# Two residual bottleneck layers on one core: VectorE's and GpSimd's order written out in one stage, beds for the kept rows, and a third term added by VectorE in another

## The chip, the cores and the metric

The kernel is one program on one core of a Trainium2 chip. The time is that of the device in microseconds; lower is better. The kernel before took 1981.97 us, the median of three runs (1979.57 to 1982.63). The profile is of one further execution.

## The reference

The input has 64 images of 1024 channels and 14 x 14 pixels, in fp32. Two layers of the same form follow each other:

```python
out = relu(bn(conv1x1(x, w1, b1)))        # 1024 -> 256 channels
out = relu(bn(conv3x3(out, w2, b2)))      # 256 -> 256
out = bn(conv1x1(out, w3, b3))            # 256 -> 1024
x = relu(x + softplus(residual_scale) * out)
```

`bn` takes mean and variance of its own input over all images and pixels, channel by channel. So no layer's result can be normalized before the whole of it, or its statistics in another way, is known.

## The kernel before

**Tiles.** Two images make a tile: 32 tiles of 392 pixels. With 128 channels on the partitions a tile of the wide tensor has 8 rows of 392 values (one row is 128 x 392), a tile of the narrow tensor 2. Tiles 16 to 31 are called kept, since their conv3 results are stored to memory (`zs`) before the normalization is known. The narrow tensor of all tiles stays on chip in `y_all`; `two(t, s)` is its area of tile t and half s.

**Products.** conv1 and conv3 use seven block products in place of eight (class `Seven`, with `Conv1` and `Conv3`). The seven, p1 to p7, use sums of weight blocks and sums t1 to t4 of the input's blocks, and their results are put together from banks of the accumulator: p1 starts a bank y, which is copied by ScalarE (`after1`), takes p6 and is copied again (`after6`), takes p7, and, in Conv3, is copied once more (`after7`, cu3). The banks are called ay, ap, ax for conv1, cy, cp, cx for conv3. `stream` puts the products of neighbouring units into this order: p1 of the unit, p3 and p4 of the unit before, p6, then `end` of the unit before, p2, p5, p7. (Conv1 has p4 before p3.) One step of a stream is two matmuls of 196 columns; a tile of conv1 has 28 steps, a unit of conv3, which makes two rows of a tile, has 7. Where the text speaks of products it means such steps.

**Stages,** by their place in the span: conv1 of the first layer (0 to 330 us); its 3 x 3 convolution, tile after tile with transformed weights (to 585); the **mixed** stage (585 to 811); the **fused** stage (811 to 1327); the 3 x 3 convolution of the second layer (to 1605); its statistics (to 1690) and the final conv3 with the residual (to 1985).

**Mixed** takes statistics of conv3's output by products of the narrow tensor with itself for tiles 0 to 15 (moves by DMA, transposes on VectorE at L1193), and makes conv3 of tiles 16 to 31 itself: class `Direct`, 60 units of two rows. A unit's row is put together in a tile `kept` and stored to `zs` by SyncE; `bn_stats` of its two rows stand in `end` (L568). In `Direct` the third term of the second row is copied from the bank by ScalarE to cu3 and added by GpSimd (L521, `after7` of `Conv3`).

**Fused** ends the first layer and makes conv1 of the second. Three generators run interleaved. *a* is conv1 of the second layer, 32 tiles in the order of `positions()`: even places are tiles 0 to 15, odd places are kept tiles. *c* is conv3 of the first layer for the tiles at even places, 60 units; one step of c follows two of a, with a start of 14 steps of c. *kept_rows* gives the 16 kept tiles their residual, row by row, 128 rows; one row every 7 steps of a, so two in a unit. Row r is loaded from `zs` by SyncE (`bring`) into a bed, a part of `y_all`, 8 rows ahead; rows 104 and later come through two beds in the raw weights, 2 ahead. Even rows of a tile are multiplied and added by VectorE in one instruction (L1689); odd rows by GpSimd in two (L1686, L1687). Then ScalarE does the relu with the shift in place. A row of a conv3 tile gets from VectorE the adds from banks cp, cy and cx (L500), from GpSimd the adds of cu12 (L526) and cu3 (L521), then the relu.

On VectorE a tile of conv1 has the block sums t3, t2, t1 (L432, L433, L434, 128 x 784) once its p1 is recorded and t4 (L451) after p6, the results (L420) and `bn_stats` (L423); each conv3 tile has four column sums (L463 to L466).

**What sets the order.** Each engine runs its instructions one after the other in a fixed list. Instructions under `tc.keep_in_program_order` stand in that list in the order in which the program records them; others are placed by a scheduler before the kernel is built. TensorE's matmuls, ScalarE's activations (`act`, L332) and SyncE's loads are under it in the fused stage; VectorE's and GpSimd's instructions there are not.

Of the kernel before, what the change touches and what calls it, by code (L numbers as in the profile page):

```python
# [69 lines left out]
def bottlenecks(ctx: ExitStack, tc: tile.TileContext, x, w1s, w2s, w3s, pars, out):  # L70
# [259 lines left out]
    def act(*args, **kw):  # L330

        tc.keep_in_program_order(nc.scalar.activation(*args, **kw))  # L332

    class Conv1(Seven):


# [37 lines left out]
        def end(self):  # L374
            pass
# [47 lines left out]
                self.run(nc.vector.bn_stats(self.stats[:, o, self.at[i % len(self.at)], :], whole), o, i)  # L423

        def run(self, ins, o, i):
            if self.pinned:
                tc.keep_in_program_order(ins)

        def after1(self):
            self.u1 = self.saved("au1")  # L430
            self.t1, self.t2, self.t3 = (self.sum(i) for i in range(1, 4))
            nc.vector.tensor_sub(self.t3, self.b[1][1], self.b[0][1])  # L432
            nc.vector.tensor_add(self.t2, self.t3, self.b[0][0])  # L433
            nc.vector.tensor_sub(self.t1, self.b[0][1], self.b[0][0])  # L434

        def after2(self):
            self.result(0, 0, self.x, self.u1)
# [10 lines left out]
        def after6(self):  # L448
            self.u2 = self.saved(*("au2",) if self.border is None else ("au4",) if len(self.ts) > 1 else ("cu3",))
            self.t4 = self.sum(4)  # L450
            nc.vector.tensor_sub(self.t4, self.b[1][0], self.t2)  # L451

        def after7(self):
            self.result(1, 1, self.p, self.saved("au3"))
# [1 line left out]
    def column_sums(pool, ys, n, twice=(2, 3), eng=nc.vector):  # L456

        sums = []
        for i in range(4):
            v = pool.tile([P, n], FP, tag=f"ct{i}", name=f"ct{i}", bufs=1 + (i in twice))  # L460
            sums.append(v.rearrange("p (h l) -> p h l", l=G * W))
        t1, t2, t3, t4 = sums
        eng.tensor_sub(t3, ys[1][1], ys[0][1])  # L463
        eng.tensor_add(t2, t3, ys[0][0])
        eng.tensor_sub(t1, ys[0][1], ys[0][0])
        eng.tensor_sub(t4, ys[1][0], t2)  # L466
        return sums

    class Conv3(Seven):
# [27 lines left out]

        def add(self, row, i, bank):
            o, v = self.o[row], self.part(row, i)
            nc.vector.scalar_tensor_tensor(v, bank, self.scale[:, o : o + 1], v, ALU.mult, ALU.add)  # L500

        def relu(self, row):
            o = self.o[row]
# [14 lines left out]

        def after7(self):
            u3 = self.saved(self.pool.tile([P, self.n], FP, tag="cu3", name="cu3", bufs=self.thirds), 1)  # L520
            nc.gpsimd.tensor_add(self.part(1, 1), self.part(1, 1), u3)  # L521

        def after3(self):
            self.add(0, 1, self.p)
            v = self.xt[:, self.o[0], :]
            nc.gpsimd.tensor_add(v, v, self.u12)  # L526

        def after4(self):
            self.add(1, 0, self.y)
# [1 line left out]
        def end(self):  # L531
            for row in range(2):
                self.relu(row)
            if self.to is not None:
                nc.scalar.dma_start(out=self.to, in_=self.xt.rearrange("p s f -> p (s f)"))

    class Direct(Conv3):

        thirds = 2

# [806 lines left out]
    def positions():  # L1347
        return [KEPT * (p % 2) + p // 2 for p in range(T)]

    def bed(r):  # L1350

        if r >= ROWS[1]:
            return None
        g, i = (NG - 3, NG - 1)[r >= ROWS[0]], r % AHEAD
        a = g * GPX + i % 4 * PX
        return y_all[:, i // 4, a : a + PX]

    def bring(to, r):

        t, o = KEPT + r // CS, r % CS  # L1360
        if t < T:
            tc.keep_in_program_order(nc.sync.dma_start(out=to, in_=zs[t - KEPT][:, o * PX : (o + 1) * PX]))

    def mixed(psum, pool, one, x_right, x_left, aff, minus_c, w3, made_c, summed_c, summed_a, mv3, xs, coming_x):

# [134 lines left out]
        places = positions()  # L1500
        for k, _ in enumerate(stream(units(), total, together=True)):
            unit, step = divmod(k, 7)
            t, q = KEPT + 1 + unit // 4, unit % 4
            if step == 0 and q == 0 and t + 1 < T:
                coming = prepare(t + 1)
            if step == 3:
                if q < 2:
                    next(coming, None)
                if q > 0:
                    next(norms, None)  # L1510
                if unit in moves:
                    move(moves[unit])
                if unit in (21, 25, 29, 33):
                    next(summed_a)
                if unit in (44, 48):
                    coming_x()
                if 50 <= unit < 50 + AHEAD:
                    bring(bed(unit - 50), unit - 50)
            if step == 5 and q == 1:
                next(coming, None)  # L1520
            if step == 2 and unit == at[0]:
                grams = batches()
            if step == 2 and unit in at or step == 5 and unit - 1 in at or step == 2 and unit - 2 in at:
                next(grams, None)
            if step == 6 and unit > at[-1] + 1:
                if tail is None:
                    assert next(grams, "end") == "end"
                    tail = conv3_stats(
                        psum, pool, (upper, lower, by, gs), w3, mv3,
                        ("ay", "ay", "ap", "ax"), homes[1], ("ay", "ay", "ay"),  # L1530
                    )
                next(tail, None)
        assert next(tail, "end") == "end"
        for _ in range(3):
            coming_x()
# [115 lines left out]
            unit.go_out()  # L1651
        residual(psum, xs[T - 1], 1, T - 1, a, aff)

    def fused(psum, pool, one, coming, xs, raw, w1, w3, aff, par, stats, border, begun):

# [4 lines left out]
        scale, shift = aff  # L1660
        n = PX // 2
        places = positions()
        beds = raw[0][:, 1, 0].rearrange("p s m -> p (s m)"), raw[1][:, 0, CS // 2 :].rearrange("p s m -> p (s m)")
        beds = [v[:, :PX] for v in beds]

        def at(r):
            return beds[r % 2] if bed(r) is None else bed(r)

        def last_convs():
            for p in range(2, T, 2):  # L1670
# [6 lines left out]
        def first_convs():  # L1677
            for p, t in enumerate(places):
                yield Conv1(psum, pool, xs[p : p + 1], (t,), w1, par, stats, border, (p,))

        def kept_rows():

            for r, (p, o) in enumerate(itertools.product(range(1, T, 2), range(CS))):
                v, z = xs[p][:, o, :], at(r)
                if o % 2:
                    nc.gpsimd.tensor_scalar(z, z, scale[:, o : o + 1], None, ALU.mult)  # L1686
                    nc.gpsimd.tensor_add(v, v, z)  # L1687
                else:
                    nc.vector.scalar_tensor_tensor(v, z, scale[:, o : o + 1], v, ALU.mult, ALU.add)  # L1689
# [6 lines left out]
                yield  # L1696

        a, c, rows = stream(first_convs(), T), stream(last_convs(), (KEPT - 1) * CS // 2), kept_rows()
        done = LAG
        for i in range(LAG):  # L1700
            next(c)
            if i == 2:
                for run in begun:
                    run()
            if i % 3 == 1:
                next(rows)
        for k in itertools.count():
            p, step = divmod(k, 28)
            if step == 14 and 0 < p < T - 4:
                assert len(xs) == p + 4  # L1710
                coming(4)
            if k % 7 == 3:
                next(rows, None)
            if next(a, "end") == "end":
                break
            while done < LAG // 2 + (k + 1) // 2:
                next(c, None)
                done += 1
        assert next(c, None) is None and next(rows, None) is None

    def stats_tile(n, name):
        return keep.tile([P, n, T, nc.vector.BN_STATS_DIM], FP, tag=f"stats{n}", name=name)
# [200 lines left out]
    for b in range(2):  # L1923
# [9 lines left out]
        with tc.tile_pool(name=f"last_{b}", bufs=1, **({"reuse_waits": "tile"} if b == 0 else {})) as one, tc.tile_pool(  # L1933
# [12 lines left out]
            with ExitStack() as scope:  # L1946
# [53 lines left out]
                with tc.tile_pool(name=f"rest_{b}", bufs=1) as pool:  # L2000
                    if b == 1:
                        final(psum, pool, [x_left] * 5 + [more], xs, w3, *weights, aff)
                        return
                    stats1 = stats_tile(MS, f"stats1_{b + 1}")
                    border = Border(b + 1, stats1, x_scope)
                    fused(psum, pool, one, coming, xs, (w1, w3), *weights, aff, par[b + 1], stats1, border, later)


# [38 lines left out]
```

## Time and profile before

| what | us |
|---|---|
| median of three runs | 1981.97 |
| the profiled execution | 1986.55 |
| its span, first to last instruction | 1984.7 |
| mixed stage, TensorE busy | 210.95 of 226.00 |
| fused, 811 to 850, TensorE busy | 34.18 of 39.00 |
| fused, 850 to 1150, TensorE busy | 283.89 of 300.00 |
| fused, 1150 to 1313, TensorE busy | 134.64 of 163.00 |
| 1313 to 1605, TensorE busy | 289.48 of 292.00 |

The profile writes PE for TensorE, PEld for its weight loads, DVE for VectorE, ACT for ScalarE, POOL for GpSimd, SP for SyncE. A timeline row has start, duration, engine, line, operation, output and input, count, and in brackets the idle time of the engine ahead of it with what ended it. Starts of rows on one engine can be closer than the durations, since one instruction begins while the one before drains. L numbers are lines of the kernel; the line of a helper stands for all that it records (L159 every matmul, L332 every activation).

### The profile page before, as it was taken

What the parts mean: (1) busy time and instruction counts of PE and PEld (TensorE: products, weight loads), DVE (VectorE), ACT (ScalarE), POOL (GpSimd) and SP (SyncE); (2) the same over time, 40 slices, a digit from 0 to 9 for tenths busy, and PEclk for the clock granted to TensorE, in tenths of its full rate; (3) what the DMA queues carried; (4) which work ended last, traced back from release to release, by engine and by line L of the source; (5) the groups of instructions that cost most, each with busy time, mean ns of one, the idle gap of its engine ahead of it and who ended that gap; (6) DMA issues with size and microseconds to landing.
All of it is one profiled execution on the core that took longest, in us unless ns stands there. A gap on an engine that the chain in (4) does not pass through costs nothing. (4 is left out here: it accounts for less than half of the span.)

```text
span 1984.7 us, 28827 instructions
## 1 busy us (share of the span) xinstructions
PE 1909.2 (96%) x9778; PEld 1576.8 (79%) x9778; DVE 1591.7 (80%) x2458; ACT 1097.2 (55%) x2283; POOL 752.6 (38%) x801
## 2 busy tenths in 40 slices
PE   9999999999998999999999997799999999999999
PEld 5555558999986788799999997789999987555555
DVE  5778669999985666888888875469999988788886
ACT  2222215777766655555455553236777783666666
POOL 0111100112125555666666644501211141667665
PEclk9999999999999999999999998899999999999999
DMA  7776735879745545777677765437787747699997
GB/s 285 280 254 237 256 122 161 223 205 222 213 142 159 159 144 203 276 272 279 260 264 272 276 235 212 159 130 212 202 225 207 204 132 257 258 324 336 344 357 277
DMA packets 246356, 458.22 MB, mean 231 GB/s; under 512 B 41344, under 2 KB 212960, under 8 KB 233152
## 3 DMA queue, kind: packets, MB, share of 16 engines
q1 hardware_dynamic: 208976, 374.23, 55.5%
q0 software_dynamic: 31616, 31.07, 7.6%
q10 hardware_dynamic: 5616, 51.06, 6.2%
q8 instruction: 78, 1.28, 0.3%
q14 instruction: 70, 0.57, 0.1%
HBM read 289.44 MB, written 141.03 MB: 217 GB/s over the span
## 5 line engine op out<-in xcount | busy, mean ns | idle before, releaser
L332 ACT ACTIVATE cu<-cy,scale 128x196 f32<-128x196 f32 (+1 forms) x360 | 178.9, 502 | 276.5 <-PE cy L159 274.6
L159 PE MATMUL columns<-v,ub 128*128 128x224 f32 (+1 forms) x1536 | 302.3, 338 | 1.1 <-ACT columns L332 0.8
L332 ACT ACTIVATE x<-x,shift 128x392 f32<-128x392 f32 x452 | 259.8, 612 | 51.2 <-POOL x L526 30.4
L159 PEld LDWEIGHTS columns<-v,ub 128*128 128x128 f32 x1536 | 268.8, 188 | 6.8 <-ACT columns L332 1.5
L159 PE MATMUL ay<-at,ws 128*128 128x196 f32 (+1 forms) x768 | 195.9, 387 | 2.6 <-ACT au L332 2.6
L159 PEld LDWEIGHTS ay<-at,ws 128*128 128x128 f32 x768 | 139.4, 194 | 37.4 <-ACT au L332 2.9
L500 DVE SCALAR_TENSOR_TENSOR x<-cp,scale,x 128x196 f32<-128x196 f32 (+1 forms) x240 | 124.1, 517 | 51.9 <-PE cp L159 50.4
L583 POOL TENSOR_TENSOR x<-x,cu 128x392 f32<-128x392 f32 x120 | 125.8, 1049 | 72.9 <-DVE x L500 71.4
L521 POOL TENSOR_TENSOR x<-x,cu 128x196 f32<-128x196 f32 (+1 forms) x120 | 121.9, 1016 | 74.6 <-ACT cu L332 66.0
L159 PE MATMUL l<-diffs,ub 128*128 128x224 f32 (+1 forms) x768 | 149.6, 337 | 0.3 <-ACT sd L1762 0.3
L159 PE MATMUL m<-sums,ua 128*128 128x224 f32 (+1 forms) x752 | 146.0, 336 | 0.2 <-DVE sums L699 0.2
L332 ACT ACTIVATE au<-ay 128x196 f32<-128x196 f32 (+1 forms) x140 | 53.2, 380 | 157.1 <-PE ay L159 149.3
L159 PEld LDWEIGHTS l<-diffs,ub 128*128 128x128 f32 x768 | 134.6, 189 | 1.2 <-ACT sd L1762 0.6
L159 PE MATMUL ap<-x,ws 128*128 128x196 f32 (+1 forms) x360 | 99.8, 410 | 37.1 <-DVE y L420 37.1
L159 PEld LDWEIGHTS m<-sums,ua 128*128 128x128 f32 x752 | 131.5, 189 | 1.4 <-DVE sums L699 0.8
L159 PE MATMUL cx<-y,w 128*128 128x196 f32 (+1 forms) x396 | 123.6, 398 | 3.5 <-DVE kept L555 3.4
L159 PE MATMUL cy<-y,w 128*128 128x196 f32 (+1 forms) x404 | 125.0, 397 | 0.0
L159 PE MATMUL cy<-ct,wt 128*128 128x196 f32 x480 | 122.7, 338 | 1.4 <-ACT cu L332 1.4
L332 ACT ACTIVATE y<-y,shift,scale 128x1568 f32<-128x1568 f32 (+7 forms) x102 | 118.7, 1183 | 6.6 <-DVE shift L1794 6.5
L997 POOL DMA_DIRECT2D y<-f x24 | 32.4, 1664 | 232.3 <-DVE f L917 232.3
L159 PE MATMUL cy<-ct,w 128*128 128x196 f32 (+1 forms) x360 | 114.1, 399 | 1.3 <-ACT cu L332 1.3
L159 PEld LDWEIGHTS ap<-x,ws 128*128 128x128 f32 x360 | 68.9, 206 | 58.0 <-DVE y L420 37.0
(298 smaller groups left out, 4448.7 us busy)
## 6 DMA issues: line engine op xcount, KB each, us to landing
ub<-u SPq DMA_DIRECT2D x92, 768.0 KB, 5.4
x<-in_x SPq DMA_DIRECT2D x35, 1568.0 KB, 8.2
x<-mid SPq DMA_DIRECT2D x32, 1568.0 KB, 8.9
mid<-x ACTq DMA_DIRECT2D x31, 1568.0 KB, 6.2
out<-x SPq DMA_DIRECT2D x123, 392.0 KB, 7.9
x<-in_x SPq DMA_DIRECT2D x108, 392.0 KB, 4.5
z<-kept SPq DMA_DIRECT2D x64, 392.0 KB, 3.0
ua<-u SPq DMA_DIRECT2D x92, 256.0 KB, 3.1
```

Source lines behind the costliest of these rows:

```text
L159: tc.keep_in_program_order(nc.tensor.matmul(*args, **kw))
L332: tc.keep_in_program_order(nc.scalar.activation(*args, **kw))
L500: nc.vector.scalar_tensor_tensor(v, bank, self.scale[:, o : o + 1], v, ALU.mult, ALU.add)
L521: nc.gpsimd.tensor_add(self.part(1, 1), self.part(1, 1), u3)
L583: nc.gpsimd.tensor_add(v, v, self.u12[:, i * self.n : (i + 1) * self.n])
L997: nc.gpsimd.dma_start(out=out_rows[3][:, o], in_=fa[:, o, :full], accum_op=ALU.add)
```

## The change

1. **Fused, order.** A list `pinned` is filled at the stage's start and emptied at its end; a helper `run` and the method `Conv1.run` put VectorE's and GpSimd's instructions under `keep_in_program_order` while it is filled. This takes in the sums, results and statistics of conv1, the column sums, the adds of conv3 and the kept rows.
2. **Fused, beds.** `bed(r)` becomes `beds(spare)`, which gives each row its bed and the row after which it is asked for. Rows 104 to 119 use the two old beds and a ring of areas of `y_all` whose tiles are done, so the eight rows of a tile are asked for together; the eight rows of the last tile come as one load into a tile `whole`.
3. **Mixed.** `Direct.after7` adds the third term straight from the bank on VectorE; cu3 and the GpSimd addition go. `bn_stats` of a unit's second row is put off to the next unit's `after7`.

The lines move: L420 to L427, L423 to L430, L432, L433, L434 to L439, L440, L441, L451 to L458, L500 to L507, L521 to L528, L526 to L533, L561 to L568, L568 to L579, L1686, L1687, L1689 to L1723, L1724, L1726. The new addition in mixed is L574.

```diff
+    pinned = []
+    def run(ins):
+        if pinned:
+            tc.keep_in_program_order(ins)
...
         def run(self, ins, o, i):
-            if self.pinned:
+            if self.pinned or pinned:
                 tc.keep_in_program_order(ins)
...
-            nc.vector.tensor_sub(self.t3, self.b[1][1], self.b[0][1])
+            run(nc.vector.tensor_sub(self.t3, self.b[1][1], self.b[0][1]))
...
     class Direct(Conv3):
-        thirds = 2
...
+        def after7(self):
+            nc.vector.tensor_add(self.part(1, 1), self.y, self.part(1, 1))
+            while waiting:
+                waiting.pop()()
+        def stat(self, row):
+            nc.vector.bn_stats(self.stats[:, self.o[row], self.t - KEPT, :], self.z[:, row])
         def end(self):
-            for row in range(2):
-                nc.vector.bn_stats(self.stats[:, self.o[row], self.t - KEPT, :], self.z[:, row])
+            self.stat(0)
+            waiting.append(partial(self.stat, 1))
...
+    def beds(spare):
+        places, before, last = [], {}, {}
+        for r in range((T - KEPT - 1) * CS):
+            t, o = KEPT + r // CS, r % CS
+            if r < ROWS[1]:
+                g, i = (NG - 3, NG - 1)[r >= ROWS[0]], r % AHEAD
+                a = g * GPX + i % 4 * PX
+                key, v = (g, i), y_all[:, i // 4, a : a + PX]
+            else:
+                ring = [(u, s) for s in range(MS) for u in range(t, T)]
+                i = o - MS
+                key = ("spare", o % MS) if i < 0 or i >= len(ring) else ring[i]
+                v = spare[key[1]] if key[0] == "spare" else two(*key)
+            places.append(v)
+            if key in last:
+                before[r] = last[key]
+            elif r >= ROWS[1]:
+                before[r] = ROWS[1] - 1
+            elif r >= AHEAD:
+                before[r] = r - AHEAD
+            last[key] = r
+        return places, before
...
             for r, (p, o) in enumerate(itertools.product(range(1, T, 2), range(CS))):
-                v, z = xs[p][:, o, :], at(r)
+                v, z = xs[p][:, o, :], at[r] if r < len(at) else whole[0][:, o]
                 if o % 2:
-                    nc.gpsimd.tensor_scalar(z, z, scale[:, o : o + 1], None, ALU.mult)
-                    nc.gpsimd.tensor_add(v, v, z)
+                    run(nc.gpsimd.tensor_scalar(z, z, scale[:, o : o + 1], None, ALU.mult))
+                    run(nc.gpsimd.tensor_add(v, v, z))
...
                 act(v, v, AF.Relu, bias=shift[:, o : o + 1])
-                for ahead in AHEAD, 2:
-                    if (r + ahead < ROWS[1]) == (ahead == AHEAD):
-                        bring(at(r + ahead), r + ahead)
+                for q in behind[r]:
+                    bring(at[q], q)
...
+            if step == 14 and p == T - 4:
+                whole.append(right.tile([P, CS, PX], FP, tag="x", name="whole"))
+                tc.keep_in_program_order(
+                    nc.sync.dma_start(out=whole[0].rearrange("p s f -> p (s f)"), in_=zs[T - 1 - KEPT])
+                )
```

More of the change, by code (lines that the diff above doesn't have):

```diff
@@ L450, in after6 @@
             self.t4 = self.sum(4)
-            nc.vector.tensor_sub(self.t4, self.b[1][0], self.t2)
+            run(nc.vector.tensor_sub(self.t4, self.b[1][0], self.t2))
         def after7(self):
@@ L462, in column_sums @@
         t1, t2, t3, t4 = sums
[L463 to L466, printed above, removed]
+        run(eng.tensor_sub(t3, ys[1][1], ys[0][1]))
+        run(eng.tensor_add(t2, t3, ys[0][0]))
+        run(eng.tensor_sub(t1, ys[0][1], ys[0][0]))
+        run(eng.tensor_sub(t4, ys[1][0], t2))
         return sums
@@ L499, in add @@
             o, v = self.o[row], self.part(row, i)
-            nc.vector.scalar_tensor_tensor(v, bank, self.scale[:, o : o + 1], v, ALU.mult, ALU.add)
+            run(nc.vector.scalar_tensor_tensor(v, bank, self.scale[:, o : o + 1], v, ALU.mult, ALU.add))
         def relu(self, row):
@@ L520, in after7 @@
             u3 = self.saved(self.pool.tile([P, self.n], FP, tag="cu3", name="cu3", bufs=self.thirds), 1)
-            nc.gpsimd.tensor_add(self.part(1, 1), self.part(1, 1), u3)
+            run(nc.gpsimd.tensor_add(self.part(1, 1), self.part(1, 1), u3))
         def after3(self):
@@ L525, in after3 @@
             v = self.xt[:, self.o[0], :]
-            nc.gpsimd.tensor_add(v, v, self.u12)
+            run(nc.gpsimd.tensor_add(v, v, self.u12))
         def after4(self):
@@ L1361, in bring @@
         if t < T:
-            tc.keep_in_program_order(nc.sync.dma_start(out=to, in_=zs[t - KEPT][:, o * PX : (o + 1) * PX]))
+            z = zs[t - KEPT][:, o * PX : (o + 1) * PX]
+            z = z if len(to.shape) == 2 else z.rearrange("p (h l) -> p h l", h=H)
+            tc.keep_in_program_order(nc.sync.dma_start(out=to, in_=z))
     def mixed(psum, pool, one, x_right, x_left, aff, minus_c, w3, made_c, summed_c, summed_a, mv3, xs, coming_x):
@@ L1499, in mixed @@
         at = [5, 9, 13, *range(16, 46, 3)]
-        places = positions()
+        at_first, _ = beds((None, None))
         for k, _ in enumerate(stream(units(), total, together=True)):
@@ L1517, in mixed @@
                 if 50 <= unit < 50 + AHEAD:
-                    bring(bed(unit - 50), unit - 50)
+                    bring(at_first[unit - 50], unit - 50)
             if step == 5 and q == 1:
@@ L1532, in mixed @@
                 next(tail, None)
+        waiting.pop()()
         assert next(tail, "end") == "end"
@@ L1652, in final, with fused @@
         residual(psum, xs[T - 1], 1, T - 1, a, aff)
-    def fused(psum, pool, one, coming, xs, raw, w1, w3, aff, par, stats, border, begun):
+    def fused(psum, pool, one, right, coming, xs, raw, w1, w3, aff, par, stats, border, begun):
         scale, shift = aff
@@ L1662, in fused @@
         places = positions()
[L1663 to L1667, printed above, removed]
+        spare = raw[0][:, 1, 0].rearrange("p s m -> p (s m)"), raw[1][:, 0, CS // 2 :].rearrange("p s m -> p (s m)")
+        at, before = beds([v[:, :PX] for v in spare])
+        behind = collections.defaultdict(list)
+        for r, q in before.items():
+            behind[q].append(r)
         def last_convs():
@@ L1696, in kept_rows @@
                 yield
+        whole = []
+        pinned.append(True)
         a, c, rows = stream(first_convs(), T), stream(last_convs(), (KEPT - 1) * CS // 2), kept_rows()
@@ L1702, in fused @@
             if i == 2:
-                for run in begun:
-                    run()
+                for late in begun:
+                    late()
             if i % 3 == 1:
@@ L1719, in fused @@
         assert next(c, None) is None and next(rows, None) is None
+        pinned.clear()
     def stats_tile(n, name):
@@ L2005, in bottlenecks @@
                     border = Border(b + 1, stats1, x_scope)
-                    fused(psum, pool, one, coming, xs, (w1, w3), *weights, aff, par[b + 1], stats1, border, later)
+                    fused(psum, pool, one, x_right, coming, xs, (w1, w3), *weights, aff, par[b + 1], stats1, border, later)
 def kernel(**inputs):
```

15 lines of the change are left out of this document (6 added, 9 removed).

## The prediction

> **What bounds the kernel now.** First the page's span, busy shares and, for later, one row of its DMA issues (count, KB, us to landing); then the windows, which give the same by stage; the columns are PE, weight load, VectorE, ScalarE, GpSimd, granted clock, DMA share and GB/s.
>
> ```profile
> span 1984.7 us, 28827 instructions
> ...
> PE 1909.2 (96%) x9778; PEld 1576.8 (79%) x9778; DVE 1591.7 (80%) x2458; ACT 1097.2 (55%) x2283; POOL 752.6 (38%) x801
> ...
> x<-in_x SPq DMA_DIRECT2D x35, 1568.0 KB, 8.2
> ```
>
> ```profile
> 585.00:811.00 226.00, 210.95 (x1327) 176.26 (x1326) 150.00 (x340) 129.90 (x361) 119.29 (x158) 0.98 0.52 168
> ...
> 850.00:1150.00 300.00, 283.89 (x1688) 280.87 (x1686) 244.08 (x421) 159.34 (x361) 191.41 (x159) 0.99 0.73 269
> 1150.00:1313.00 163.00, 134.64 (x709) 131.28 (x708) 96.18 (x186) 67.18 (x152) 71.78 (x63) 0.88 0.51 185
> ```
>
> TensorE is the bound nearly everywhere; only where it idles can a change win, and only work put on its path can lose. The diff touches two stages. Mixed (585 to 811) leaves TensorE idle for 226.00 - 210.95 = 15.05 us in all. Fused is told best by its products. These are its first and last rows on TensorE, and around 1026 the products of conv3 (two records each):
>
> ```profile
> 816.59 0.49 PE L159 MATMUL cy<-y,w 128*128 128x196 f32 x2
> ```
>
> ```profile
> 1325.47 1.49 PE L159 MATMUL ay<-x,ws 128*128 128x196 f32 x8
> ```
>
> ```profile
> 1026.93 0.49 PE L159 MATMUL cp<-y,wt 128*128 128x196 f32 x2
> ...
> 1031.91 0.49 PE L159 MATMUL cy<-ct,wt 128*128 128x196 f32 x2
> ...
> 1032.90 0.49 PE L159 MATMUL cy<-y,w 128*128 128x196 f32 x2
> ...
> 1033.90 0.49 PE L159 MATMUL cp<-y,wt 128*128 128x196 f32 x2
> ...
> 1039.56 0.49 PE L159 MATMUL cp<-ct,wt 128*128 128x196 f32 x2
> ```
>
> The interleave is one conv3 product after two of conv1, so between the rows at 1026.93 and 1031.91 lie five conv3 and ten conv1 products: 4.98 / 15 = 0.332 us for each. The stage has 60 units of 7 conv3 products and 32 tiles of 28 conv1 products, 420 + 896 = 1316, or 437 us; it lasts 1325.47 + 1.49 - 816.59 = 510.4. So **about 73 us are lost**. The waits of the steady part (850 to 1150) and of the late part (1150 to 1310), as total, times, longest, say where:
>
> ```profile
> PE ap L159 <- DVE y L420: 16.1, 10, 2.5
> ...
> ACT x L332 <- POOL x L526: 8.9, 24, 0.5
> ```
>
> ```profile
> DVE x L1689 <- DMA w<-z: 29.2, 11, 6.5
> POOL w L1686 <- DMA w<-z: 27.7, 10, 6.9
> ...
> PE ap L159 <- DVE y L420: 20.0, 6, 7.2
> ```
>
> Steady: a stall of 1.6 us once in two tiles, 16.1 in all. Late: VectorE and GpSimd wait for the rows that come through two beds, TensorE behind them (20.0 there), and the clock falls: (1 - 0.88) x 163 = 20 us. The rest, some 17, is the stage's start and single gaps.
>
> **The change, part by part.**
>
> *The beds (fused).* Eight areas instead of two let rows 104 and later be asked for early, and the last tile comes whole. This takes the late waits away: 20.0 of stalls, some 20 of clock and a few single gaps, up to 45 us. On SyncE's queue it moves the eight loads and the whole tile's ahead of what used to stand between them. The eight are asked for only when row 103 is done: the longest late wait for a bed, 6.9 us, is the nearest row, so 0 to 7 us once. The whole tile, 1568 KB, lands after some 8.2 us by the page's row of that size; its first use is ten conv1 products on, 15 products or 5.0 us at today's pace, so 0 to 3 us once. I take 0 for both, since the parts below leave each load more time than it has now.
>
> *The pinned order (fused).* TensorE's and ScalarE's orders here are the same as before, so what counts is what stands ahead of what on VectorE and GpSimd. Here is one unit on GpSimd and on ScalarE as it runs now:
>
> ```profile
> 1029.98 1.26 POOL L1686 TENSOR_SCALAR y<-y,scale 128x392 f32<-128x392 f32 x1
> 1031.33 1.50 POOL L1687 TENSOR_TENSOR x<-x,y 128x392 f32<-128x392 f32 x1
> 1032.81 1.98 POOL L1686 TENSOR_SCALAR y<-y,scale 128x392 f32<-128x392 f32 x1
> ...
> 1038.00 1.02 POOL L526 TENSOR_TENSOR x<-x,cu 128x392 f32<-128x392 f32 x1 [0.42 <-DVE x L500]
> ```
>
> ```profile
> 1029.45 0.42 ACT L332 ACTIVATE cu<-cy,scale 128x196 f32<-128x196 f32 x1 [2.05 <-PE cy L159]
> ...
> 1031.44 0.33 ACT L332 ACTIVATE au<-ay 128x196 f32<-128x196 f32 x1 [0.40 <-PE cp L159]
> ...
> 1038.10 0.42 ACT L332 ACTIVATE cu<-cy,scale 128x196 f32<-128x196 f32 x1 [3.07 <-PE cy L159]
> 1039.05 1.13 ACT L332 ACTIVATE x<-x,shift 128x392 f32<-128x392 f32 x2 [0.53 <-POOL x L526]
> ```
>
> Now two odd kept rows run one after the other on GpSimd (L1686 at 1029.98 and again at 1032.81). They run ahead of need: ScalarE's relu of an odd row stands in its fixed order between the two copies of a unit into cu12, and no wait of that relu for L1687 is in either list above; its only GpSimd wait is for L526 (8.9 us, relus at a unit's end). In the recorded order each unit has on GpSimd: the add of cu3, the add of cu12 of the unit before (L526, new L533), then the odd row's multiplication and addition (new L1723, L1724). On ScalarE: first cu12 copy, relu of that same row, second cu12 copy. TensorE may not put the seventh product on bank cy until the second copy has read it. A loop closes, once in each of the 60 units:
>
> p3 on cp, then VectorE's add from cp (L507), GpSimd's L533, L1723, L1724, ScalarE's relu and second copy, then p7.
>
> TensorE leaves 4.98 us from p3 to p7 (1026.93 to 1031.91). The loop, by rows:
>
> ```profile
> 1030.98 0.97 DVE L434 TENSOR_TENSOR at<-x 128x784 f32<-128x784 f32 x1
> ...
> 1032.53 1.13 DVE L432 TENSOR_TENSOR at<-x 128x784 f32<-128x784 f32 x1
> 1033.59 0.95 DVE L1689 SCALAR_TENSOR_TENSOR x<-y,scale,x 128x392 f32<-128x392 f32 x1
> 1034.46 0.96 DVE L433 TENSOR_TENSOR at<-at,x 128x784 f32<-128x784 f32 x1
> ...
> 1037.05 0.55 DVE L423 BATCH_NORM_STATS2 stats<-y 128x6 f32<-128x392 f32 x1
> 1037.53 0.40 DVE L500 SCALAR_TENSOR_TENSOR x<-cp,scale,x 128x196 f32<-128x196 f32 x1
> ...
> 1040.09 0.42 DVE L500 SCALAR_TENSOR_TENSOR x<-cp,scale,x 128x196 f32<-128x196 f32 x1 [0.57 <-PE cp L159]
> ```
>
> The row at 1039.56 on TensorE that released 1040.09 is the same step as p3: 0.53 from a product's start to the add's. The add takes 0.40 and GpSimd starts 0.07 later (1037.53, 1038.00); L533 1.02, L1723 1.26, L1724 1.02 as L526 of the same shape, 0.13 between them; relu 0.5 (half of a pair's 1.13), copy 0.42, with 0.11 of hand-overs. Sum **5.5 us**, 0.5 more than there is, with GpSimd undisturbed. The rows at 1032.81 and 1031.33 are the high end: 1.98 and 1.50, so 6.7.
>
> *Two halves of a tile.* That is the half in which the add from cp is next on VectorE. In the other half its recorded place is behind the three column differences of the next conv1 tile. From the moment R at which the second copy ends, ScalarE does two relus (1.1) and au3 (0.33; with a store's issue between in some, 0.4 more). VectorE's first instruction there waits for au3; then come, at the starts' spacing of the rows, result 0.33, two adds 0.66, kept row 0.62 to 0.95, three differences 0.9 to 1.1 each, statistics 0.5 and the add from cp 0.41: 5.2 to 5.8. So the add ends at R + 6.7 to 7.2, and the loop from there (L533 on) takes 4.5 to 5.7: this half lasts 11.2 to 12.9 us, where TensorE needs 7.0. In the first half p3 starts two steps of 1.0 us after p7, so R + 2.0 + 5.5 = 7.5 to 9.1.
>
> *Clock.* A long gap also costs rate afterwards:
>
> ```profile
> 1202.79 1.65 PE L159 MATMUL ap<-x,ws 128*128 128x196 f32 x4 [3.19 <-DVE y L420]
> ```
>
> ```profile
> 1066.43 0.93 PE L159 MATMUL ap<-x,ws 128*128 128x196 f32 x4 [2.49 <-DVE y L420]
> ```
>
> Four records took 1.65 us after a gap of 3.19, but 0.93 after one of 2.49. A gap of 4 to 6 us in each tile would so halve the rate for some 5 us; where the loop, not TensorE, sets the time, only the 2.0 us from p7 to p3 grow, to 4.0. I take 0 to 2 us for a tile and 0.7, because the gap may come in two pieces. [...]
>
> *Sum for fused.* A tile takes 11.7 + 7.6 + 0.7 = **20.0 us** (ends: 18.7 and 24), where its 42 products need 14.0. The loop runs while conv3 does, (420 - 14) / 14 = 29 tiles: 29 x 6.0 = 174 us lost, and I leave 7 for start and tail. Lost now: 73. So **+108 us**. The late waits and the steady stall are inside the 73 that go.
>
> *Mixed.* Per unit a ScalarE copy and a GpSimd addition go, a VectorE addition from the bank comes, and the statistics of the second row wait for the next unit. Rows of that stage:
>
> ```profile
> L332 ACT ACTIVATE cu<-cy 128x196 f32<-128x196 f32 x180 | 55.8, 333 | 5.1 <-POOL kept L521 1.4 <-PE cy L159 1.2
> ...
> L521 POOL TENSOR_TENSOR kept<-kept,cu 128x196 f32<-128x196 f32 x60 | 35.9, 599 | 61.1 <-ACT cu L332 59.3 <-DVE mv L1970 1.8
> ...
> L159 PE MATMUL cp<-ct,wt 128*128 128x196 f32 x120 | 31.9, 347 | 1.9 <-DVE kept L561 1.9
> L159 PE MATMUL cx<-y,w 128*128 128x196 f32 x120 | 30.7, 338 | 3.5 <-DVE kept L555 3.4
> ...
> L561 DVE TENSOR_TENSOR kept<-cp,cu 128x196 f32<-128x196 f32 x60 | 21.3, 355 | 39.3 <-PE cp L159 38.6
> ```
>
> Away: 60 copies of 333 ns (a third of the 180), 60 additions of 599 ns, 20 and 36 us on engines with room (129.90 and 119.29 busy of 226). Added: 60 of some 355 ns, 21 us on VectorE, which is 150.00 busy. What can hurt is that the next product on that bank now waits for VectorE, with transposes and other work queued ahead. Ends: nothing hidden, +21; all idle TensorE time won, -15. The like waits that VectorE causes today are 1.9 (cp) and 3.5 (cx): I take their sum, **+5**.
>
> Span 1984.7 + 108 + 5 = 2097.7. The profiled execution was 1986.55, 1.85 above its span, so 2099.5; the median 1981.97 is 4.6 lower, so about **2095 us**.
>
> **Rivals.**
> 1. *Heavier loop.* VectorE and GpSimd disturb each other throughout, and the clock falls after every gap: 12.9, 8.1 (the middle of 7.5 to 9.1 is 8.3) and 2.0, 23 us for a tile, 29 x 9 + 7 - 73 + 5 = +200, **2182**. For it: the 1.98 of L1686, with VectorE busy beside it. Against: in the loop VectorE stands idle while GpSimd works.
> 2. *Half a loop.* The long half is shorter, since the differences fill VectorE while it would wait anyway: 16 to 17.5 us for a tile, 58 to 101 + 7 - 73 + 5, so -3 to +41, **1979 to 2023**. For it: with no rows ahead, the kept row of VectorE may be done before au3.
> 3. *Faster.* The relu isn't late: if p3 to the second copy stays under 4.98 us in both halves, nothing holds p7, the steady stall goes (its VectorE order is other) and so do the late waits: 73 falls to some 13, **1927** with the mixed price. It decides at 4.98 us; the rows give 5.5, and the long half has the differences in front as well. Against it too: the rule that ScalarE runs in its order is not in doubt.
> 4. *It doesn't do what it says.* The eight rows and the whole tile land late: 7 + 3 us on top of any of these, which moves no chance by much (**2105** with the forecast).
>
> **How the numbers follow.** Forecast 0.67 (18.7 to 22 us for a tile: 2058 to 2153), heavier 0.10, half 0.12, faster 0.11. A measurement of this kernel tells 0.2%, 4 us, from no change; of the half loop 0.02 falls there and 0.01 below. So faster 0.12, same 0.02, slower 0.86. The range leaves out the faster case, the lower third of the half loop (0.04) and the top of the heavier (0.05): **2000 to 2185**.
>
> **What would show it.** Right: a wait of ScalarE's relu for GpSimd's L1724 and of GpSimd's L533 for VectorE's L507, about 60 times and tens of us each; two gaps of TensorE in a tile, at cy behind ScalarE's cu, the long one in the half with the differences; granted clock under 0.9 in the windows of 850 to 1150; no late waits for DMA from z. Wrong: a fused stage under 500 us, no wait for L1724, or a tile period near 14 us. For mixed: TensorE's wait on cy for VectorE's new addition, near 5 us in all.

## The result and the profile after

The changed kernel takes 2121.07 us (median of four runs, 2118.72 to 2123.52) against 1980.77 for the kernel before on the same chips: a ratio of 1.071, 95% interval 1.069 to 1.073. That is 140 us slower; 114 slower had been forecast (2095, range 2000 to 2185).

The span grew from 1984.7 to 2116.9, by 132.2 us (the two profiled executions took 1986.55 and 2118.72 us). These are the first and last products of the fused stage, as in the prediction for before:

```profile
816.78 0.49 PE L159 MATMUL cy<-y,w 128*128 128x196 f32 x2
```

```profile
1457.56 1.49 PE L159 MATMUL ay<-x,ws 128*128 128x196 f32 x8
```

1457.56 + 1.49 - 816.78 = 642.3 us, where it was 510.4: 131.9 of the 132.2 are in this stage. Its waits from 850 to 1430 (in the lines: total, times, longest), and the windows, mixed first (columns as before: PE, weight load, VectorE, ScalarE, GpSimd, granted clock, DMA share, GB/s):

```profile
ACT x L332 <- POOL x L1724: 296.1, 57, 5.6
POOL x L528 <- ACT cu L332: 247.9, 57, 5.7
DVE y L427 <- ACT au L332: 137.7, 28, 5.3
...
POOL x L533 <- DVE x L507: 94.2, 56, 2.8
PE cy L159 <- ACT cu L332: 91.8, 38, 3.1
```

```profile
585.00:811.00 226.00, 211.80 (x1324) 172.64 (x1325) 165.96 (x398) 114.67 (x300) 85.38 (x98) 1.00 0.52 167
850.00:1150.00 300.00, 238.81 (x1228) 222.36 (x1228) 164.50 (x311) 109.49 (x264) 122.05 (x119) 0.92 0.55 195
```

ScalarE's relu now waits for GpSimd's row addition in 57 units, 5.2 us on the mean; no such wait was there before. Every engine in the loop waits for the one ahead of it, and TensorE, last, for ScalarE's copy: 91.8 us there, in 38 waits, beside the 111.8 of its weight loads. The stall of TensorE behind VectorE's L427 (then L420) and all but 0.4 us of waits for rows from memory are gone from that part.

One turn of the loop, engine by engine, in the half of a tile with the three differences. VectorE first:

```profile
1049.75 0.42 DVE L427 SCALAR_TENSOR_TENSOR y<-ap,par,au 128x196 f32<-128x196 f32 x1 [4.55 <-ACT au L332]
...
1050.75 0.62 DVE L1726 SCALAR_TENSOR_TENSOR x<-y,scale,x 128x392 f32<-128x392 f32 x1
1051.28 0.97 DVE L439 TENSOR_TENSOR at<-x 128x784 f32<-128x784 f32 x1
...
1053.18 1.37 DVE L441 TENSOR_TENSOR at<-x 128x784 f32<-128x784 f32 x1
...
1054.95 0.40 DVE L507 SCALAR_TENSOR_TENSOR x<-cp,scale,x 128x196 f32<-128x196 f32 x1
...
1058.09 1.11 DVE L1726 SCALAR_TENSOR_TENSOR x<-y,scale,x 128x392 f32<-128x392 f32 x1
```

GpSimd, which takes the row up behind the cu12 addition:

```profile
1055.43 1.01 POOL L533 TENSOR_TENSOR x<-x,cu 128x392 f32<-128x392 f32 x1 [1.71 <-DVE x L507]
1056.42 1.26 POOL L1723 TENSOR_SCALAR y<-y,scale 128x392 f32<-128x392 f32 x1
1057.77 1.01 POOL L1724 TENSOR_TENSOR x<-x,y 128x392 f32<-128x392 f32 x1
```

ScalarE, with the second copies (cu) at 1048.05 and 1059.34:

```profile
1048.05 0.42 ACT L332 ACTIVATE cu<-cy,scale 128x196 f32<-128x196 f32 x1 [0.40 <-PE cp L159]
...
1058.81 0.62 ACT L332 ACTIVATE x<-x,shift 128x392 f32<-128x392 f32 x1 [5.62 <-POOL x L1724]
1059.34 0.41 ACT L332 ACTIVATE cu<-cy,scale 128x196 f32<-128x196 f32 x1
1059.64 1.12 ACT L332 ACTIVATE x<-x,shift 128x392 f32<-128x392 f32 x2
1060.67 0.32 ACT L332 ACTIVATE au<-ay 128x196 f32<-128x196 f32 x1
```

And TensorE's p7 of this unit and of the next:

```profile
1059.80 0.60 PE L159 MATMUL cy<-ct,wt 128*128 128x196 f32 x2 [2.94 <-ACT cu L332]
...
1068.24 0.49 PE L159 MATMUL cy<-ct,wt 128*128 128x196 f32 x2
```

The copy at 1048.05 frees p7. VectorE, idle since 1045.20, waits on until au3 comes (1049.75; 4.55 us in all, 1.70 of them behind the copy), does its block, and ends the add from cp at 1055.35; GpSimd's three operations follow without a gap to 1058.78; the relu (after 5.62 us of waiting), the copy at 1059.34, and TensorE goes on at 1059.80 after 2.94 us with nothing to do. From copy to copy: 1059.34 - 1048.05 = 11.29. Over the stage this is 11.29 and 11.79 by turns. On GpSimd the rows (L1724) come 11.79 us and, in the other half, 7.50 or 9.84 us after one another, but for three short halves of 8.9 to 9.1.

### The profile page after: what moved, and what is told of

Its sections match the earlier page's. It is cut to its first block, busy times and chain, and to the rows that moved or that the text cites. A ratio compares the mean times of both kernels' runs of the same rounds, so it can differ in the third digit from the quotient of the medians.

```text
span 2116.9 us, 28631 instructions
## 1 busy us (share of the span) xinstructions
PE 1963.2 (93%) x9778; PEld 1602.9 (76%) x9778; DVE 1586.6 (75%) x2518; ACT 1068.3 (50%) x2223; POOL 680.7 (32%) x741
## 3 DMA queue, kind: packets, MB, share of 16 engines
q8 instruction: 78, 1.28, 0.3%
## 5 line engine op out<-in xcount | busy, mean ns | idle before, releaser
L332 ACT ACTIVATE cu<-cy,scale 128x196 f32<-128x196 f32 (+1 forms) x360 | 173.1, 498 | 108.0 <-PE cy L159 100.2
L159 PE MATMUL cy<-ct,wt 128*128 128x196 f32 x480 | 132.1, 359 | 95.3 <-ACT cu L332 93.9
L528 POOL TENSOR_TENSOR x<-x,cu 128x196 f32<-128x196 f32 (+1 forms) x120 | 118.3, 986 | 270.2 <-ACT cu L332 261.6
L507 DVE SCALAR_TENSOR_TENSOR x<-cp,scale,x 128x196 f32<-128x196 f32 (+1 forms) x240 | 124.1, 517 | 71.5 <-PE cp L159 70.4
L159 PEld LDWEIGHTS cy<-ct,wt 128*128 128x128 f32 x480 | 83.6, 198 | 112.0 <-ACT cu L332 108.9
L427 DVE SCALAR_TENSOR_TENSOR y<-ap,par,au 128x196 f32<-128x196 f32 (+1 forms) x90 | 43.0, 478 | 144.7 <-ACT au L332 144.2
L159 PE MATMUL cy<-y,w 128*128 128x196 f32 (+1 forms) x404 | 129.8, 411 | 0.0
L159 PE MATMUL ay<-at,w 128*128 128x196 f32 (+1 forms) x376 | 97.4, 389 | 13.5 <-ACT au L332 13.5
```

Source lines behind the costliest of these rows:

```text
L159: tc.keep_in_program_order(nc.tensor.matmul(*args, **kw))
L427: self.run(nc.vector.scalar_tensor_tensor(y, ps, bias, more, ALU.add, ALU.add), o, i)
L507: run(nc.vector.scalar_tensor_tensor(v, bank, self.scale[:, o : o + 1], v, ALU.mult, ALU.add))
L528: run(nc.gpsimd.tensor_add(self.part(1, 1), self.part(1, 1), u3))
```

## The experiments

All eleven are variants of the changed kernel except where the text says otherwise. Times are medians; a ratio is to the kernel before, run beside it, with its interval.

**Cut the loop at GpSimd.** The odd row's two operations are recorded with the even row before:

```diff
-                if o % 2:
-                    run(nc.gpsimd.tensor_scalar(z, z, scale[:, o : o + 1], None, ALU.mult))
-                    run(nc.gpsimd.tensor_add(v, v, z))
+                if o % 2 == 0:
+                    v1, z1 = area(r + 1, p, o + 1)
+                    run(nc.gpsimd.tensor_scalar(z1, z1, scale[:, o + 1 : o + 2], None, ALU.mult))
+                    run(nc.gpsimd.tensor_add(v1, v1, z1))
```

> The changed kernel, but GpSimd's two operations of each odd kept row are recorded half a unit earlier, with the even row before it; the relu stays in its place. Theory (the loop p3, add from cp, L533, L1723, L1724, relu, second copy, p7 sets the pace): the loop is cut, no wait of ScalarE's relu for GpSimd's row addition is left above a few us, a tile takes 14 to 15 us in place of 20.5, and the time is 1925 to 1950 us. Rival (VectorE's recorded order, with the add from cp behind three differences, costs by itself): the long half stays near 11 us and the time above 2050.

**Cut it at ScalarE.** The relu of an odd row is recorded at the next row's place:

```diff
-                act(v, v, AF.Relu, bias=shift[:, o : o + 1])
+                held.append((v, p, o))
+                if o % 2 == 0:
+                    close(*held.pop())
...
                 yield
+                if o % 2:
+                    close(*held.pop())
```

> The changed kernel, but ScalarE's relu of an odd kept row is recorded at the next row's place, half a unit later, behind the second copy; GpSimd's and VectorE's orders stay. Theory of the loop: cut at its other end, so again 1925 to 1955 us; GpSimd's row now has the time up to the next half. Rival (GpSimd's recorded order costs by itself, since its cu12 addition waits for VectorE and the row stands behind it): TensorE still waits, above 2050.

Measured: 1935.64 (ratio 0.977, 0.974 to 0.980) and 1931.09 (0.975, 0.973 to 0.977). The windows 850 to 1150 of the two:

```profile
850.00:1150.00 300.00, 298.40 (x1783) 294.96 (x1782) 235.66 (x450) 159.59 (x381) 174.03 (x170) 1.00 0.79 282
```

```profile
850.00:1150.00 300.00, 297.41 (x1778) 294.07 (x1777) 232.95 (x445) 161.56 (x380) 173.45 (x171) 1.00 0.78 284
```

TensorE is busy 298.40 and 297.41 of 300 us where the changed kernel has 238.81, and the clock is full. In the second, ScalarE still waits for the row, but behind the copy that TensorE needs, and that costs TensorE almost nothing (L1731 is the row addition in this build):

```profile
ACT x L332 <- POOL x L1731: 31.8, 42, 1.0
...
PE cy L159 <- ACT cu L332: 2.6, 11, 0.4
```

Half a unit on either side of the loop is worth 185 to 190 us, and a tile takes 14.1 to 14.2 us in place of 20.5 (by GpSimd's rows), as expected. The rival, that VectorE's order costs by itself, falls: that order is untouched in both. So does the rival that GpSimd's order costs by itself, since it is untouched in the second.

**A longer loop.** One more GpSimd multiplication by 1.0 in each odd row:

```diff
                     run(nc.gpsimd.tensor_scalar(z, z, scale[:, o : o + 1], None, ALU.mult))
+                    run(nc.gpsimd.tensor_scalar(z, z, 1.0, None, ALU.mult))
```

> The changed kernel with one more GpSimd multiplication (by 1.0, 1.26 us and 0.08 of hand-over) in each odd kept row, inside the loop. If the loop sets the pace everywhere, each of some 58 halves grows by 1.34: +78 us, 2199. The gap of TensorE in the long half grows from 2.94 to some 4.3 us: if the clock then falls after each of them, where it now falls after every other, 14 more short halves last 2.3 longer: +33, 2232. If the loop isn't the bound: under 2150.

Measured: 2207.46, 86 us over the changed kernel. One unit's row on GpSimd, the fourth and the 62nd row addition, and the window:

```profile
1008.20 1.26 POOL L1723 TENSOR_SCALAR y<-y,scale 128x392 f32<-128x392 f32 x1
1009.55 1.19 POOL L1724 TENSOR_SCALAR y<-y 128x392 f32<-128x392 f32 x1
1010.83 1.01 POOL L1725 TENSOR_TENSOR x<-x,y 128x392 f32<-128x392 f32 x1
```

```profile
848.53 1.02 POOL L1725 TENSOR_TENSOR x<-x,y 128x392 f32<-128x392 f32 x1
```

```profile
1525.38 1.01 POOL L1725 TENSOR_TENSOR x<-x,whole 128x392 f32<-128x392 f32 x1
```

```profile
850.00:1150.00 300.00, 219.53 (x1095) 206.17 (x1094) 145.94 (x275) 97.09 (x234) 137.73 (x129) 0.90 0.49 175
```

The extra operation takes 1.28 (1010.83 - 1009.55). From GpSimd's fourth row addition to its 62nd, 58 halves, it is 1525.38 - 848.53 = 676.85 us, where the changed kernel has 594.36 (its two rows stand in the next part): 82.5 more, of which 58 x 1.28 make 74. The long halves grew by 1.28 on the mean, the short ones by 1.57; the 8 us over are in the short halves, as falls of the clock would put them, and the granted clock is 0.90 in place of 0.92. So what is put into the loop is paid in full, once a unit. The extra fall of the clock came to about a quarter of what the expectation allowed.

**One engine's order at a time.** In the first run only GpSimd's order is recorded in the fused stage, in the second only VectorE's; the other's instructions lose `run(...)`.

> The changed kernel, with VectorE's order in the fused stage left to the scheduler again, GpSimd's recorded. Theory: the loop closes over GpSimd, so it stays: 2060 to 2125 us, with the long half a little different where the scheduler puts the add from cp. Rival (VectorE's order is the cause): below 1960.

> The changed kernel, with GpSimd's order in the fused stage left to the scheduler again, VectorE's recorded. Theory: GpSimd's rows run ahead again, the relu finds them done, 1925 to 1960 us. Rival (VectorE's order is the cause): above 2060.

Measured, the first: 2112.08 (1.066, 1.062 to 1.071), as the loop has it. The wait stays (850 to 1150):

```profile
ACT x L332 <- POOL x L1724: 157.0, 29, 7.7
```

The second gave 2009.03 (1.014, 1.010 to 1.018), a miss for both theories. The relu no longer waits for L1724, but relus wait for the cu12 addition L533, and in SyncE's list (the second fence) loads of rows (L1396) wait for VectorE (both 850 to 1330):

```profile
ACT x L332 <- POOL x L533: 122.8, 30, 11.6
...
POOL y L1723 <- DMA y<-z: 97.4, 39, 10.7
```

```profile
SPq L1396 <- DVE x L1726: 138.6, 20, 13.3
```

In GpSimd's list the scheduler again puts the odd rows further ahead: before the 30th cu12 addition stand 33 of them, where the changed kernel has 31. (The expectation of the next run says some six rows ahead; counted so, it is two odd rows, about four rows, more than in the changed kernel.) L1723 then waits 97 us for its load. SyncE issues the loads of even and odd rows in one list, and waits there 139 us for VectorE's even rows, whose beds are to be used again and which now stand at their recorded place. The cu12 addition L533 stands behind L1723 on GpSimd, and ScalarE behind L533. In the run without any recorded order (below) GpSimd's rows stand just as far ahead, SyncE doesn't wait for L1726, and L1723 waits little (850 to 1310):

```profile
POOL y L1723 <- DMA y<-z: 15.0, 14, 3.3
```

So the waits for loads need both, rows that far ahead on GpSimd and VectorE's recorded order. To test the distance, GpSimd's rows were recorded seven ahead (up to row 103), all orders recorded:

```diff
+                    until = max(r + 1, min(r + EARLY_ROWS, ROWS[1] - 1))
+                    while done_odd[0] + 2 <= until and 1 + 2 * ((done_odd[0] + 2) // CS) < len(xs):
+                        done_odd[0] += 2
...
+                        run(nc.gpsimd.tensor_scalar(z1, z1, scale[:, o1 : o1 + 1], None, ALU.mult))
+                        run(nc.gpsimd.tensor_add(v1, v1, z1))
```

> As the run with GpSimd's odd row recorded earlier, but seven rows ahead in place of one, up to row 103, as far as the loads allow. It tests why VectorE's recorded order alone left 2009 us: there the scheduler has GpSimd's rows some six ahead, L1723 waits 97 us for its load, and the cu12 addition stands behind it. By that, with rows seven ahead the waits for the load come back (over 30 us in all) and the time is 1950 to 2010. Rival (it was something else in that order): no waits for loads, 1930 to 1940.

Measured: 1989.85 (1.006, 1.004 to 1.009), with the waits for loads and for SyncE's list behind VectorE that the explanation asks for (in this build L1723 is L1736, L1726 L1738, L533 L534, and ScalarE's helper L333; 850 to 1330):

```profile
POOL y L1736 <- DMA y<-z: 113.1, 16, 12.6
ACT x L333 <- POOL x L534: 97.0, 29, 9.0
```

```profile
SPq L1397 <- DVE x L1738: 123.4, 19, 11.2
```

So with all orders recorded the distance has two ends: none closes the loop (2121), one row opens it (1936), seven run into the loads (1990). How much of the 2009 is due to the distance alone isn't shown.

**The parts alone.** First the changed kernel without `pinned.append(True)`: beds and mixed stage, the fused order left to the scheduler.

> The changed kernel without any recorded order on VectorE and GpSimd in the fused stage: the beds and the mixed stage alone. Theory: the late waits for rows go (20 us of stalls, some 20 of clock), mixed costs about 1, so 1940 to 1965 us. Rival (the late rows were hidden, or the eight loads at once land late): 1975 or more.

Measured: 1955.43 (0.988, 0.985 to 0.990). Then the later relu with the two old beds, `bed` and `bring` as before:

```diff
-                for q in behind[r]:
-                    bring(at[q], q)
+                for ahead in AHEAD, 2:
+                    if (r + ahead < ROWS[1]) == (ahead == AHEAD):
+                        bring(at(r + ahead), r + ahead)
```

> The kernel with the later relu, but with the beds of the kernel before (two beds, two rows ahead, from row 104 on). It tells what the beds are worth once the loop is cut. By the late part of before (20 us of stalls, 20 of clock): 1960 to 1975, that is 30 to 45 us over the 1931 of the later relu. Rival (the late waits came from the scheduler's order, which asks for rows too late, and not from the number of beds): 1930 to 1940.

Measured: 1939.70 (0.981, 0.979 to 0.982), 9 us over the same kernel with the new beds, not 30 to 45; by the ratios, 0.981 and 0.975, some 12. The rival is nearer: with the recorded order little waits for loads even with two beds (L1712 is the multiplication of a row in a bed of the raw weights):

```profile
POOL w L1712 <- DMA w<-z: 9.9, 4, 5.4
```

9.9 us are left of the 27.7 that GpSimd waited there in the kernel before, and of VectorE's 29.2 nothing is left. Where the scheduler sets the order the beds and the mixed part are worth 23 us, so most of the late waits are an effect of two beds and that order together.

**The mixed part.** The kernel before with the mixed part alone, and the later relu with the old mixed part:

```diff
+        def after7(self):
+            nc.vector.tensor_add(self.part(1, 1), self.y, self.part(1, 1))
+            while waiting:
+                waiting.pop()()
...
+            self.stat(0)
+            waiting.append(partial(self.stat, 1))
```

> The kernel before with only the mixed stage's part: the third term added by VectorE from the bank, the second row's statistics put off. By the two profiles (mixed 231.3 us against 230.4) it costs 1 us: 1980 to 1984. The prediction's price was +5; a rival is a gain of up to 5 that the changed kernel's trace hides at the stage's end.

> The kernel with the later relu, but with the mixed stage of the kernel before. It prices the mixed part where the fused stage has no late loads to blur it. From the profiles of the stage (230.7 to 231.3 us new, 230.4 old): 1930 to 1931, within 0.1% of the later relu. Rival (the new addition saves what the alone run hints, 2.6 us): 1933 to 1934. The prediction's +5: 1926.

Measured: 1975.39 against 1978.0 (0.9983, 0.9971 to 0.9996), and 1929.22 (0.976, 0.974 to 0.978) where the new mixed part has 1931.09 (0.975) beside another run of the kernel before. By the medians the new part takes 2.6 us less in the first pair and 1.9 more in the second, which ran on different chips; by the ratios, which take out the chips, it takes 0.17% and 0.1% less. The interval of the first pair is 0.04% to 0.29% less; those of the second overlap, so that it shows no difference. So the part is worth between nothing and a gain of 0.3%, and not the +5. In the changed kernel TensorE waits for the new addition (585 to 816):

```profile
DVE kept L574 <- ACT kept L332: 32.0, 28, 2.7
...
PE cy L159 <- DVE kept L574: 6.1, 10, 1.1
```

6.1 us of new waits, about the +5 of the prediction, but the stage's TensorE is busy 211.80 of 226.00 where it was 210.95: the waits for L555 (3.4) and others went. Why the run alone gains as much as it does stays open: its mixed stage lasted 230.7 us by its trace, 230.4 before, so the gain isn't there. In the two traces the difference stands in the fused stage, 494.4 us (from 816.72 to the end of the row at 1309.66) against 510.4, with a granted clock of 0.94 from 1150 to 1313 where it was 0.88; but these are single executions, 15.3 us apart, where the medians are 2.6 apart.

**Both cuts.** GpSimd's row earlier and the relu later:

> Both cuts together: GpSimd's odd row half a unit earlier and its relu half a unit later. In the two single cuts ScalarE still waits a little for the row (42 us in 56 waits where the relu is later) or relus follow late loads. If those waits hold TensorE anywhere, both cuts give 1925 to 1930; if TensorE's remaining idle time is the stage's start alone, the time stays at 1930 to 1936.

Measured: 1931.84 (0.977, 0.976 to 0.978), as with the later relu alone.

```profile
811.00:850.00 39.00, 34.33 (x171) 30.00 (x171) 27.61 (x53) 20.15 (x44) 23.09 (x21) 0.96 0.68 253
850.00:1150.00 300.00, 298.14 (x1780) 294.41 (x1779) 232.52 (x443) 160.98 (x383) 175.22 (x171) 1.00 0.78 285
1150.00:1270.00 120.00, 116.88 (x695) 114.53 (x694) 91.83 (x181) 57.88 (x139) 60.63 (x59) 1.00 0.73 245
```

Nothing is left to win in the loop: in the 300 steady us TensorE idles for 1.9. What it still loses is at the stage's ends, 39.00 - 34.33 = 4.7 us at the start and 3.1 in the last window.

## Why the prediction was right, point by point

- **The loop** is as told, and the cuts show that it is the cause: relu behind L1724, L1724 behind L533, L533 behind the add from cp, p7 behind the second copy. Undoing it at either end takes 185 to 190 us off, lengthening it by 1.28 us adds that once in every half.
- **The signs**: the relu's waits for L1724 came 57 times and L533's for L507 56 times, and the late waits for rows went. Of the two gaps at cy in a tile only the long one came; in the short half TensorE waits at ay, behind ScalarE's au and relu, for 1.1 us at most (850 to 1430):

```profile
PE ay L159 <- ACT au L332: 13.5, 28, 0.6
...
PE ay L159 <- ACT x L332: 11.6, 14, 1.1
```

- **The long half**: 11.7 forecast from copy to copy, 11.29 and 11.79 measured by turns (11.79 on GpSimd's rows). VectorE's block took 5.6 us (1049.75 to 1055.35), GpSimd's three operations 1.01, 1.26 and 1.01, as the undisturbed rows said. The high end (1.98, 1.50) didn't come, but not for the reason that the prediction gave against a heavier loop. VectorE stands all but idle beside GpSimd's three operations only in the short half (busy for 0.42 of their 3.35 us, once for 0.80); in the long half it is busy all through them (3.31 to 3.33 us), in every such turn from 850 to 1430, and they take no longer (1.01, 1.26 and 1.01 in both halves). Beside L1724 it was VectorE's row that got longer: L1726 took 1.11 us there (1058.09) and 0.62 with GpSimd idle (1050.75). So the price was right and the reason for it half wrong: luck. Two small sums were off as well, without effect on the forecast: the terms of VectorE's block add up to 6.15 at their high end, not 5.8, and those of the first half to 2.0 + 6.7 = 8.7, not 9.1. And the product at 1039.56, read as the same step as p3, is p5, which goes to the same bank.
- **The short half**: 7.5 by the rows, 7.6 in the sum; 7.50 measured with the full clock (granted: 1.00 from 1059.80 to 1066.20).
- **The clock** is the term that was too small. I had taken 0.7 us a tile, an estimate from the two rows at 1202.79 and 1066.43; no run shows it. The short half mostly alternates between 7.50 and 9.84, so 2.3 us about every other tile (in 16 of 29 it was lengthened), 1.2 on the mean. I had the size of one fall (2.0) nearly, but not how often. The gap came in pieces, as I had allowed, the largest of 2.94 (3.12 once), but such pieces cost the rate too: behind the one that ends at 1079.08 the granted clock was 0.50 from 1079 to 1085. In the kernel before it was 0.50 from 1202.79 to 1208.10, behind the gap of 3.19, which is the 5 us of half rate that I had counted with. The granted clock in the window was 0.92, not under 0.9.
- **The tile**: GpSimd's fourth row addition begins at 840.72, its 62nd at 1435.08: 58 halves or 29 tiles in 594.4 us, 20.5 each, against 20.0. 29 x 0.5 = 15 us.
- **Start and tail**: 642.3 - 594.4 for the other 1316 - 29 x 42 = 98 products, which need 32.5: 15 us lost, not 7.

The two rows of GpSimd (new L1724) that bound the 58 halves:

```profile
840.72 1.01 POOL L1724 TENSOR_TENSOR x<-x,y 128x392 f32<-128x392 f32 x1
```

```profile
1435.08 1.01 POOL L1724 TENSOR_TENSOR x<-x,whole 128x392 f32<-128x392 f32 x1
```

These two terms, 15 + 8, are nearly the whole of what the sum for fused missed, 131.9 against 108. Two smaller terms and the rivals:

- **The beds**: the late waits went, as told, and the eight loads at once cost nothing that shows (0.4 us of waits for rows from 850 to 1430). But the 45 us that I gave to the two beds were mostly an effect of beds and order together; with the loop cut the beds bring 9 to 12.
- **Mixed**: +5 forecast, 0 to a gain of 0.3% measured.
- **The rivals**: the faster case was the one to be had by half a unit's shift: 1927 forecast for a loop that doesn't hold p7, 1931 measured once it doesn't.

## What to carry to other kernels

Writing down the order in which a program records its instructions takes away the slack by which a scheduler had let one engine run ahead; before pinning, follow each wait of the pinned engines around and see whether the chain comes back to the engine that started it within one turn. If it does, compare its length with the turn of the engine that bounds the kernel. Here moving one small group by half a unit was worth 185 to 190 us, and each microsecond put into the loop was paid in full (58 times 1.28 us cost 82.5). The slack had an upper end too: rows recorded seven ahead waited for their loads (113.1 us), with others queued behind them.

## What was not expected of the hardware

The clock did not go by the length of the gap alone. Each long half of the changed kernel leaves TensorE idle for the same 2.94 us (2.92 to 2.95 in 28 of the 29 from 850 to 1430); after the one at 1059.80 (above) two records took 0.60 us, after the next they took 1.02, and the half rate (0.86 for two records, where 0.49 is usual; a granted clock of 0.50 from 1079 to 1085) stayed for some 6 us:

```profile
1079.08 1.02 PE L159 MATMUL cy<-ct,wt 128*128 128x196 f32 x2 [2.94 <-ACT cu L332]
1079.89 1.51 PE L159 MATMUL ax<-x,w 128*128 128x196 f32 x4
1081.20 0.86 PE L159 MATMUL cy<-y,w 128*128 128x196 f32 x2
```

It went on in turns, one tile at the full rate and one with the fall (three times over the stage two falls followed each other), and two tiles take 1100.71 - 1059.80 = 40.91 us:

```profile
1100.71 0.60 PE L159 MATMUL cy<-ct,wt 128*128 128x196 f32 x2 [2.94 <-ACT cu L332]
```

What makes the turns is not shown: no run here changes the length of the gap, or its place in time, alone. In the kernel before, too, the length alone did not decide: a gap of 2.49 us left the rate alone (the row at 1066.43 in the prediction: 0.93 for four records), and a shorter one of 2.13 did not (1.54 for four, and a granted clock of 0.52 from 1245.89 to 1249.10):

```profile
1245.89 1.54 PE L159 MATMUL ap<-x,ws 128*128 128x196 f32 x4 [2.13 <-DVE y L420]
```
